# A graph layer's edge sum on one core: two quads of edges are summed behind all other late nodes instead of one, the lists are cleared in 4 transfers instead of 14

## The chip, the core and the metric

The kernel runs on one core of a Trainium2 chip. Five engines work side by side, each on its own queue in order: PE (matrix products), DVE (elementwise work and reductions), ACT (activation functions), POOL (here almost only gathers by index) and SP (here only issues transfers). PE writes to PSUM, of which the program keeps four banks in a list. The metric is the time of one execution in microseconds; lower is better.

## The reference

One layer of a message-passing network over 12,500 nodes with 128 features and 400,000 edges, sorted by destination, then a residual and a layer norm:

```python
rbf = exp(-(distances[:, None] - centers) ** 2 / (2.0 * width * width))
cut = 0.5 * (cos(pi * distances / CUTOFF) + 1.0) * (distances <= CUTOFF)
W = (silu(rbf @ fw1 + fb1) @ fw2 + fb2) * cut[:, None]
messages = (h[src] @ pw + pb) * W
agg = segment_sum(messages, dst, num_segments=num_atoms)
y = h + (silu(agg @ mw1 + mb1) @ mw2 + mb2)      # h is x
out = layernorm(x + y)                           # so layernorm(2 x + ...)
```

Edges whose length is over the cutoff add nothing, so the kernel first packs the others into lists.

## The kernel before

**Quads.** The packed edges are worked in 139 quads (`NL`) of 512 edges. Quad `q` goes through: four gathers of 128 rows each on POOL (`fetch`, L1074; in eight quads, `SINGLY`, one of the four is copied row by row by SP instead); a radial basis and a first product for two quads together (`basis`, `first`, `silu`, on ACT and PE); a second product into a PSUM bank (`second`, L1144 and L1147); DVE's product of that bank and the gathered rows (`message`, L1156 and L1158); a one-hot matrix of destinations (`place`, L1170); PE's product of both, which is the sum over edges (`sum_up`, L1190); and DVE's addition into the table `aggT` at a base that is read from a list (`add`, L1223). A quad of the first four lists has one window of sums, one of the later lists two, of 128 nodes at most.

**Nodes.** A group of up to four tiles of 128 nodes can be finished once all edges to it have been added: `node_first` (two products into a bank, L1233 and L1234, then silu on ACT, L1238), `node_second` (L344 and L347), `node_stats` on DVE (L1254, L1259), `deviations` (four small DVE instructions and a square root, L1266 to L1270), `scales` (L1277, L1278), `normalize` (L1289 on DVE or POOL, L1292 on ACT) and a store. A late node group is named by its first tile: 80 and 84 have four tiles, 88 two, 90 three, 93 two, 95 three (the last cut off at 84 nodes).

**The last quad.** The quads are not taken in the order of their lists. `quad_of` takes one quad out of the third list and puts it last: quad 138 of the order is number 26 of the lists (`LAST`). Its edges end in early nodes, and where the data allow it only in one tile of them, `END` (tile 3). So every node but those of `END` is complete before it, and after it only `END` has to be finished.

**Order.** The code is one long program, in which each engine executes its instructions as they were written. The main loop takes step `q` from 0 to 136: message, work on nodes (`nodes`), `second(q + 2)`, the sum, the bases, the one-hot of the next quad, the additions that `added` gives out, and `tail`. `tail` and `READY` say how many steps before the end each late group has its `node_first`. `last_step` writes out the two last quads by hand, the very last in four pieces of 128 edges, each multiplied and summed as its gather lands.

**Banks.** `bank()` takes the first bank of a list and `free.append` gives it back when the code that uses it has been written, not when it has run. Where three of the four banks are in use, the next user gets the bank that was just given back, and waits at run time for whatever still reads it.

```python
    def bank(own=None):
        while not free:
            go_on(next(c for c in held if c != own))
        return free.pop(0)
```

**Lists.** Before the packing scatters (L507) the lists in memory are cleared by SP (`clear_packed`, L229): 5 transfers, then 3, then 6.

Of the kernel before, what the change touches and what calls it, by code (L numbers as in the profile page):

```python
# [43 lines left out]
NL = 139  # L44
LAST = 26
AHEAD = 3
# [24 lines left out]
EARLY_US = 7  # L71
SINGLY = (22, 44, 62, 67, 86, 102, 118, 133)
A_ROW = .58
# [5 lines left out]
TAIL = {80: 4, 84: 4, 88: 2, 90: 3, 93: 2, 95: 3}  # L79
READY = {80: 9, 84: 6, 88: 5, 90: 4}  # L80
END = 3
# [5 lines left out]
def kernel(  # L87
# [60 lines left out]

    def load_x(t0, n=None):
        t = x4_sb[loaded[0] % X_BUFS]  # L150
        loaded[0] += 1
        node_dma(t0, t, x, False, n)
        x_sb[t0] = t
# [26 lines left out]
    def quad_of(q):  # L180

        return q if q < LAST or q >= NL else LAST if q == NL - 1 else q + 1

    def steps(k):

        return k if k <= LAST or k >= NL else k - 1

# [35 lines left out]
    def clear_packed(k, eng):  # L223
        a, b = CLEAR[k:k + 2]
        for i in range(LISTS if k == 0 else 3):
            v = packed[i, a:b].rearrange("(p w) -> p w", p=P)
            for w0 in range(0, (b - a) // P, 376):
                n = min(376, (b - a) // P - w0)
                eng.dma_start(v[:, w0:w0 + n], zero_i[:, :n])  # L229

# [593 lines left out]
    def unpack(c):  # L824
# [132 lines left out]
        if QB[c] <= LAST < QB[c + 1]:  # L957
            k = 2 * (LAST - QB[c])
            upto, that = (work.tile([64, 1], F32, name=n, bufs=1)[:np_] for n in ("upto", "that"))
            nc.vector.scalar_tensor_tensor(that, ident[:np_, k:k + 1], -1.0, ident[:np_, k + 1:k + 2],  # L960
                                           op0=OP.mult, op1=OP.subtract)
# [122 lines left out]
    def quads(o):  # L1084

        return [q for q in (2 * o, 2 * o + 1) if q < NL]

    def radial(o, lengths, eng=nc.sync):

        n = math.prod(lengths.shape) // QE  # L1090
        d = work.tile([P, QE], F32, name="d", bufs=3)
        v = lengths.rearrange("(o h) e -> o h e", o=1)
        eng.dma_start(d, v.to_broadcast([64, 2, QE]))
        d_of[o] = d, n

    next_o = [0]

    def radials(to):

        while next_o[0] < min(to, -(-NL // 2)):  # L1100
            o = next_o[0]
            if not all(chunk_of(q) in stored for q in quads(o)):
                break
            a, b = 2 * quad_of(quads(o)[0]), 2 * quad_of(quads(o)[-1]) + 2
            assert b - a == 2 * len(quads(o))
            radial(o, near_d[a:b].rearrange("(h t) e -> h (t e)", t=2))
            next_o[0] += 1
# [97 lines left out]

    def bases_of(q0, q1):

        _, v = nc.values_load_multi_w_load_instructions(
            base_i[0:1, 2 * quad_of(q0):2 * quad_of(q1 - 1) + 2], engines=[mybir.EngineType.DVE],
            min_val=0, max_val=N - min(wide(q) for q in range(q0, q1)),  # L1210
            skip_runtime_bounds_check_because="bases are destinations, and end in the table")
        for k in range(2 * (q1 - q0)):
            bases[q0 + k // 2, k % 2] = v[k]

    def added(q):

        return max((q - 2) // 2 * 2 if q < NL - 14 else q - 1 if q < NL - 4 else q, 0)

# [84 lines left out]
    def finish(every):  # L1303

        for t0 in every:
            load_x(t0)
# [5 lines left out]
            normalize(*ready.pop(0), on=range(QT))  # L1312

# [32 lines left out]
    def nodes(q):  # L1346
# [21 lines left out]
        if q == NL - 7:  # L1368
            st_of[3] = statistics()
            node_stats(80, st_of[3])  # L1370
        if q == NL - 4:
            node_stats(84, st_of[3][:, 4:])
        if q == NL - 3:
            node_stats(88, st_of[3][:, 8:])

    st_of, deep = {}, []

    def last_step(q, msg):

        assert not ready and not deep and not singles  # L1380
        bases_of(q, NL - 1)
# [6 lines left out]
        assert done_to(2 * q + 2) >= 95 * P  # L1388
        node_first(93)

# [5 lines left out]
        add(q)  # L1396
        node_first(95)
        last(1)
        normalize(*ready.pop(0))
        for n in (2, 3):  # L1400
            normalize(*ready.pop(0), on=range(n), v=nc.gpsimd)
        node_second(93)
        last(2)
        node_second(95)
        last(3)
        node_stats(93, st_of[1], lambda: add(NL - 1))
        node_first(END)
        node_stats(95, st_of[1][:, 2:])
        node_second(END)
        node_stats(END, st_of[1][:, 5:])  # L1410
        scales(*deviations([93, 95, END], st_of[1]))
        normalize(*ready.pop(0), on=(0, 1), v=nc.gpsimd)
        normalize(*ready.pop(0), on=(0, 1), eng=nc.scalar)
        normalize(*ready.pop(0), on=(0,))
        assert not ready

    def tail(q):

        for t0, k in READY.items():
            if q == NL - k:  # L1420
                assert done_to(2 * added(q + 1) + (2 if t0 > 88 else 0)) >= (t0 + TAIL[t0]) * P
                node_first(t0)
# [144 lines left out]
    for q in range(NL - 2):  # L1567
# [33 lines left out]
        if q == NL - 3:  # L1601
            st_of[1] = statistics()
            node_stats(90, st_of[3][:, 10:])
        if q == NL - 4:
            place(NL - 1)
            base_of(NL - 1)
            node_dma(END, end_sb, x, False)
            x_sb[END] = end_sb
        for k in now:
# [19 lines left out]
        elif counted and some is None and fetched[0] >= QT * NL:  # L1629
            some = nc.values_load(bad_i[0:1, 2:3], min_val=0, max_val=3 * E)  # L1630
    last_step(NL - 2, message(NL - 2))

    def more(q):

        fetch(-2, srci[:, 2 * q:2 * q + 2, :].rearrange("p r j -> p (r j)"))
        radial(-1, near_d[2 * q:2 * q + 2].rearrange("(o p) e -> o (p e)", o=1))
        basis(-1)
# [11 lines left out]
    def everything():  # L1649
        nc.vector.memset(aggT, 0.0)  # L1650
        def again(e0, seen):
# [20 lines left out]
            fetch(-2, idx)  # L1672
            radial(-1, edge_weight[ds(e0, QE)].rearrange("(o e) -> o e", o=1), nc.gpsimd)
            basis(-1)
# [64 lines left out]
```

## Time and profile before

| | us |
|---|---|
| three runs | 719.8, 721.39, 721.6 (median 721.39) |
| the profiled execution | 719.15 |
| its span, first to last instruction | 717.5 |
| busy in the span: PE, DVE, POOL, ACT | 590.3, 561.8, 536.4, 397.3 |

The profiled execution is 1.65 us longer than its span, and lies 2.24 us under the median of the runs. In the rows of the timeline the first number is the start in us from the span's start, the second the length; "x8" counts instructions merged into a row; a bracket gives the idle time ahead of it and what ended it.

### The profile page before, as it was taken

The page shows a single profiled execution, that of the slowest core. Times are in us where ns is not written, and L with a number is a line of the kernel's source. Part 1 is how long each engine was busy: PE and PEld are TensorE (multiplying, and loading weights), DVE is VectorE, ACT ScalarE, POOL GpSimd, SP SyncE. Part 2 cuts the span into 40 slices and gives each one's busy share as a digit, 9 for nine tenths or more (in the row PEclk, how much of TensorE's full clock was granted, in tenths as well). Part 3 has the DMA queues.
Part 4 walks back from the last instruction along what each step waited for, and adds up shares of the span by engine and source line. Part 5 has one row for each costly group of instructions (what it writes and reads, how often), then busy time and mean ns, then how long its engine had stood idle before and what let it go on. Part 6 is the DMA issues. An engine that isn't in the chain of part 4 may idle for free. (4 is left out here: it accounts for less than half of the span.)

```text
span 717.5 us, 13667 instructions
## 1 busy us (share of the span) xinstructions
PE 590.3 (82%) x3524; PEld 465.0 (65%) x3524; DVE 561.8 (78%) x1736; ACT 397.3 (55%) x564; POOL 536.4 (75%) x576
## 2 busy tenths in 40 slices
PE   6887877898889889888588896999987878878884
PEld 5775556776667667576466674787765655656663
DVE  8899799787988999899689895878655455565685
ACT  6557624563645566464348253858744833574474
POOL 7777777777777777777777777777777777777773
PEclk9999687997988999999979997999998999999998
DMA  8995442343334334343333343444433433244342
GB/s 263 348 324 174 149 128 75 87 137 100 98 86 121 97 95 108 97 128 83 94 106 113 98 119 103 137 127 135 136 97 99 148 92 114 84 141 134 96 130 91
DMA packets 53389, 91.35 MB, mean 127 GB/s; under 512 B 13856, under 2 KB 21120, under 8 KB 53306
## 3 DMA queue, kind: packets, MB, share of 16 engines
q1 hardware_dynamic: 34754, 53.20, 22.9%
q0 software_dynamic: 17840, 36.77, 19.8%
q8 instruction: 29, 0.48, 0.3%
q10 hardware_dynamic: 712, 0.46, 0.2%
q14 instruction: 54, 0.44, 0.2%
HBM read 74.59 MB, written 15.79 MB: 126 GB/s over the span
## 5 line engine op out<-in xcount | busy, mean ns | idle before, releaser
L1074 POOL DMA_INDIRECT quad<-proj,srci x421 | 400.6, 952 | 128.4 <-issue 97.6
L1147 PEld LDWEIGHTS bank<-fw_sb,s 128*128 128x128 f32 x1112 | 160.8, 208 | 66.5 <-issue 59.8
L1136 ACT ACTIVATE s<-ph 128x1024 f32<-128x1024 f32 x70 | 71.3, 1018 | 184.4 <-PE ph L1130 184.3
L1147 PE MATMUL bank<-fw_sb,s 128*128 128x128 f32 x1112 | 161.8, 293 | 0.0
L1130 PE MATMUL ph<-rbf,w_sb 102*128 102x512 f32 x278 | 147.1, 655 | 7.5 <-ACT rbf L1122 3.9
L1190 PEld LDWEIGHTS sums<-hot,msg 128*128 128x128 f32 x816 | 112.0, 204 | 54.9 <-issue 27.4
L1170 DVE TENSOR_SCALAR hot<-iota_n,dl,cut 128x80 f32<-128x80 f32 (+4 forms) x408 | 110.1, 344 | 23.6 <-PE sums L1190 21.7
L1190 PE MATMUL sums<-hot,msg 128*128 128x80 f32 (+4 forms) x816 | 113.7, 285 | 15.4 <-DVE msg L1156 7.7
L1144 PE MATMUL bank<-fb_b,ones_b 96*128 96x512 bf16 x139 | 56.1, 404 | 48.8 <-DVE msg L1158 29.8
L1074 POOL DMA_INDIRECT x<-proj,srci x79 | 75.0, 949 | 24.1 <-issue 19.8
L1158 DVE TENSOR_TENSOR msg<-bank,quad 128x512 f32<-128x512 f32 (+1 forms) x82 | 55.7, 679 | 39.4 <-DMA quad<-proj,srci 36.9
L1130 PEld LDWEIGHTS ph<-rbf,w_sb 102*128 102x128 f32 x278 | 52.8, 211 | 48.1 <-issue 38.8
L1223 DVE TENSOR_TENSOR aggT<-aggT,sums 128x80 f32 (+4 forms) x209 | 54.0, 258 | 32.5 <-PE bank L1234 11.7
L1121 ACT ACTIVATE rbf<-d,rbf_bias,rbf_scale 102x512 f32<-102x512 f32 x70 | 56.2, 803 | 14.8 <-DMA d<-near_d 14.7
L1074 POOL DMA_INDIRECT quad<-in_x_dram,srci x48 | 47.6, 992 | 14.8 <-issue 11.9
L347 PEld LDWEIGHTS bank<-pw_sb,xT 128*128 128x128 f32 (+1 forms) x292 | 42.0, 207 | 8.0 <-issue 4.0
L1122 ACT ACT_TABLE_LOAD x35 | 44.9, 1283 | 0.6
L1136 ACT ACT_TABLE_LOAD x35 | 44.9, 1283 | 0.6
L1122 ACT ACTIVATE rbf<-rbf 102x512 f32<-102x512 f32 x70 | 44.1, 630 | 1.5
L1190 PE MATMUL sums<-quad,quad 128*128 128x104 f32 (+3 forms) x296 | 40.9, 281 | 3.9 <-DVE quad L1158 3.9
L1170 DVE TENSOR_SCALAR quad<-iota_n,dl,cut 128x104 f32<-128x104 f32 (+3 forms) x148 | 40.5, 348 | 3.9 <-issue 2.8
L1158 DVE TENSOR_TENSOR quad<-bank,quad 128x512 f32<-128x512 f32 (+2 forms) x40 | 25.2, 632 | 23.4 <-DMA quad<-proj,srci 16.1
(282 smaller groups left out, 803.0 us busy)
## 6 DMA issues: line engine op xcount, KB each, us to landing
d<-near_d SPq DMA_DIRECT2D x70, 256.0 KB
dl<-proj SPq DMA_DIRECT2D x1024, 0.5 KB
x<-in_x_dram SPq DMA_DIRECT2D x45, 256.0 KB
quad<-proj,srci POOLq DMA_INDIRECT x421
proj<-hp SPq DMA_DIRECT2D x24, 256.0 KB
out_dram<-x SPq DMA_DIRECT2D x21, 256.0 KB
r_d<-in_edge_weight_dram SPq DMA_DIRECT2D x5, 256.0 KB
r_dst<-in_dst_dram SPq DMA_DIRECT2D x5, 256.0 KB
```

The lines of the kernel that those rows point to most:

```text
L347: nc.tensor.matmul(to[:m, k, :], lT[:, k * P:k * P + m], w, start=False, stop=(k == a + c - 1))
L1074: ins = nc.gpsimd.indirect_dma_start(out=got[:, j, :], out_offset=None, in_=proj if table is None else table, in_offset=bass.IndirectOffse ...
L1121: nc.scalar.activation(rbf[:u], d[:u], AF.Square, bias=rbf_bias[:u], scale=rbf_scale[:u])
L1122: nc.scalar.activation(rbf[:u], rbf[:u], AF.Exp, scale=-1.0 / (2.0 * width * width))
L1130: nc.tensor.matmul(ph[:, h, :], w1_sb[:2 * KR, h, :], rbf[:2 * KR], start=True, stop=True)
L1136: nc.scalar.activation(s[:, :n], ph[:, :n], AF.Silu)
L1144: nc.tensor.matmul(pu, ones_b[:, :P], bias_b["fb2"].rearrange("k j f -> k (j f)"), start=True, stop=False)
L1147: nc.tensor.matmul(pu[:, j * H:(j + 1) * H], s[:, j * P:(j + 1) * P], fw2_sb, start=False, stop=(j == QT - 1))
L1158: nc.vector.tensor_mul(msg[:, a:b, :], pu_of[q].rearrange("p (j f) -> p j f", j=QT)[:, a:b, :], got_of[q][:, a:b, :])
L1170: nc.vector.tensor_scalar(hot[:, j, :wide(q)], iota_n[:, :wide(q)], dl[:, at[0], at[1]], cut[:, at[0], at[1]], op0=OP.is_equal, op1=OP.mult)
L1190: ins = nc.tensor.matmul(pa[:, k * W:k * W + wide(q)], msg[:, j, :], hot[:, j, :wide(q)], start=(j % n == 0), stop=(j % n == n - 1))
L1223: nc.vector.tensor_add(to, to, pa[:, k * W:k * W + wide(q)])
```

## The change

- Two quads, numbers 25 and 26 of the lists, now come last (`N_LAST = 2`, as quads 137 and 138); every other quad from 25 on moves up by one place. Both have one window of 80 nodes. Their edges that go beyond `END` would be counted as misses, as before for one.
- So all late nodes are complete after quad 136. `READY` starts group 84 one step earlier, 88 and 90 too, and 93 and 95, which were in `last_step`, in the main loop. Statistics and second products move with them.
- `last_step` has one set of `deviations` over the 14 tiles of 84, 88, 90, 93 and 95, ahead of quad 137's sum. After the last quad only `END` is left: its double input is added by PE into the bank, the statistics are taken from the bank, and a `bn_aggr` replaces the four small instructions.
- `END`'s input is loaded one step earlier, and doubled by ACT in place.
- The lists are cleared by one transfer for all lists together: 1, then 1, then 2.
- Three numbers in `SINGLY` follow the shifted order. In code that runs only when edges were missed, transfers move from SP's queue to POOL's.

```diff
-LAST = 26
+LAST = 25
+N_LAST = 2
-READY = {80: 9, 84: 6, 88: 5, 90: 4}
+READY = {80: 9, 84: 7, 88: 6, 90: 5, 93: 4, 95: 3}
...
-        return q if q < LAST or q >= NL else LAST if q == NL - 1 else q + 1
+        late = q - (NL - N_LAST)
+        return q if q < LAST or q >= NL else LAST + late if late >= 0 else q + N_LAST
...
-        for i in range(LISTS if k == 0 else 3):
-            v = packed[i, a:b].rearrange("(p w) -> p w", p=P)
-            for w0 in range(0, (b - a) // P, 376):
-                n = min(376, (b - a) // P - w0)
-                eng.dma_start(v[:, w0:w0 + n], zero_i[:, :n])
+        m = LISTS if k == 0 else 3
+        v = packed[:m, a:b].rearrange("s (p w) -> p s w", p=P)
+        for w0 in range(0, (b - a) // P, 376):
+            n = min(376, (b - a) // P - w0)
+            eng.dma_start(v[:, :, w0:w0 + n], zero_i[:, None, :n].to_broadcast([P, m, n]))
...
-        return max((q - 2) // 2 * 2 if q < NL - 14 else q - 1 if q < NL - 4 else q, 0)
+        return max((q - 2) // 2 * 2 if q < NL - 14 else q - 1 if q < NL - 5 else q, 0)
...
-    def last_step(q, msg):
+    def last_step(q):
...
-        roots = deviations([84, 88, 90], st_of[3][:, 4:])
+        node_second(95)
+        node_stats(95, st_of[1][:, 11:])
+        msg = message(q)
+        nc.scalar.activation(warm, half_pi, AF.Sqrt)
+        roots = deviations([84, 88, 90, 93, 95], st_of[1])
         nc.scalar.activation(warm, half_pi, AF.Silu)
...
-        keep_busy(5)
+        keep_busy(3)
         sum_up(q, msg)
...
         scales(*roots)
         add(q)
-        node_first(95)
+        keep_busy(2)
         last(1)
...
+        normalize(*of[95], on=range(3))
+        normalize(*of[88])
+        normalize(*of[90])
+        keep_busy(2)
         last(2)
+        normalize(*of[93], on=range(2))
+        normalize(*of[84], on=range(4), v=nc.gpsimd)
+        keep_busy(1)
+        pz, py = bank(), bank()
...
+        nc.tensor.matmul(py[:, :H], ident, end_sb[:, 0, :], start=False, stop=False)
         last(3)
+        add(NL - 1)
+        nc.tensor.matmul(pz[:, :P], mw1_sb, aggT[:, END * P:(END + 1) * P], start=False, stop=True)
...
+        nc.scalar.activation(zs, pz[:, :P], AF.Silu)
+        nc.tensor.matmul(py[:, :H], zs, mw2_sb, start=False, stop=True)
...
+        nc.vector.bn_stats(st, py[:, :H])
+        nc.vector.bn_aggr(mv, st)
...
+        nc.scalar.activation(dev[:, 0:1], mv[:, 1:2], AF.Sqrt, bias=eps)
+        nc.vector.reciprocal(dev[:, 1:2], dev[:, 0:1])
+        nc.vector.tensor_scalar(end_sb[:, 0, :], py[:, :H], mv[:, 0:1], dev[:, 1:2],
+                                op0=OP.subtract, op1=OP.mult)
...
+        node_dma(END, end_sb, out, True)
...
         if q == NL - 4:
             keep_busy(2)
+            node_second(90)
         if q == NL - 3:
-            node_second(90)
+            node_second(93)
...
+        if q == NL - 5:
             node_dma(END, end_sb, x, False)
-            x_sb[END] = end_sb
+            nc.scalar.activation(end_sb, end_sb, AF.Copy, scale=2.0)
```

What this moves on the engines is seen in three places.

On PE, around the sums of quads 132 and 133 (the two rows `sums<-hot`), before: `fb_b` and `fw_sb` mark the second product of a quad, `aggT,mw_sb` the first product of a node group, here of group 84.

```order
L1190 MATMUL sums<-hot_1071,msg_1076 128x128 x4
L1144 LDWEIGHTS ones_b
L1144 MATMUL bank_169<-fb_b,ones_b 128x512
L1147 MATMUL bank_169<-fw_sb,s 128x128 x4
L1130 MATMUL ph<-rbf,w_sb 128x512
L1190 MATMUL sums<-hot_1190,msg_1218 128x128 x4
L1233 LDWEIGHTS mb_b
L1233 MATMUL bank_170<-ones_b,mb_b 128x512
L1234 MATMUL bank_170<-aggT,mw_sb 128x512
```

The same place now:

```order
L1197 MATMUL sums<-hot_1065,msg_1070 128x128 x4
L1231 LDWEIGHTS mb_b
L1231 MATMUL bank_169<-ones_b,mb_b 128x512
L1232 MATMUL bank_169<-aggT,mw_sb 128x512
L1151 LDWEIGHTS ones_b
L1151 MATMUL bank_169<-fb_b,ones_b 128x512
L1154 MATMUL bank_169<-fw_sb,s 128x128 x4
L1137 MATMUL ph<-rbf,w_sb 128x512
L1197 MATMUL sums<-hot_1184,msg_1208 128x128 x4
```

Group 84's first product has moved from behind quad 133's sum to ahead of quad 135's second product, which uses the same bank (`bank_169`) right after it.

On ACT, from the square roots ahead of the last groups on, now (`zs` are the silus of groups 88 and 90, `x` the tiles that are normalized, `end` the tile of `END`):

```order
L1631 ACT_TABLE_LOAD
L1631 ACTIVATE warm<-half_pi 128x1
L1236 ACTIVATE zs<-bank_167 128x256
L1290 ACTIVATE x_89<-x_89,by,rs 128x128 x4
L1290 ACTIVATE x_90<-x_90,by,rs 128x128 x4
L1625 ACTIVATE end<-end 128x128
L1236 ACTIVATE zs<-bank_170 128x384
L1290 ACTIVATE x_91<-x_91,by,rs 128x128 x4
```

Before, the first silu here was group 84's, group 88's stood in the place of the `end` row, and group 90's behind eight more normalized tiles.

On SP, the transfers of that time, now:

```order
L179 DMA out_dram<-x_89 128x512
L179 DMA out_dram<-x_90 128x512
L179 DMA x_89<-in_x_dram 128x256
L179 DMA end<-in_x_dram 128x128
L179 DMA out_dram<-x_91 128x512
L179 DMA out_dram<-x_92 128x512
```

`END`'s load has moved from behind all loads of the late groups to behind the load into `x_89`, which waits until that tile's store, two rows above, has landed.

More of the change, by code (lines that the diff above doesn't have):

```diff
@@ L71 @@
 EARLY_US = 7
-SINGLY = (22, 44, 62, 67, 86, 102, 118, 133)
+SINGLY = (22, 43, 62, 66, 86, 102, 118, 133)
 A_ROW = .58
@@ L1088, in radial @@
     def radial(o, lengths, eng=nc.sync):
-        n = math.prod(lengths.shape) // QE
         d = work.tile([P, QE], F32, name="d", bufs=3)
-        v = lengths.rearrange("(o h) e -> o h e", o=1)
-        eng.dma_start(d, v.to_broadcast([64, 2, QE]))
-        d_of[o] = d, n
+        for h, v in enumerate(lengths):
+            v = v.rearrange("(o h) e -> o h e", o=1)
+            if len(lengths) == 1:
+                eng.dma_start(d, v.to_broadcast([64, 2, QE]))
+            else:
+                eng.dma_start(d[h::2], v[:, 0, :].to_broadcast([64, QE]))
+        d_of[o] = d, sum(math.prod(v.shape) for v in lengths) // QE
     next_o = [0]
@@ L1204, in base_of @@
             bases[q, k] = v[0]
[L1206 to L1213, printed above, removed]
     def added(q):
-        return max((q - 2) // 2 * 2 if q < NL - 14 else q - 1 if q < NL - 4 else q, 0)
+        return max((q - 2) // 2 * 2 if q < NL - 14 else q - 1 if q < NL - 5 else q, 0)
     def add(q, ks=(0, 1)):
@@ L1305, in finish @@
         for t0 in every:
[L1306 removed]
+            load_x(t0, eng=nc.gpsimd)
             st = statistics()
@@ L1311, in finish @@
             scales(*deviations([t0], st))
-            normalize(*ready.pop(0), on=range(QT))
+            normalize(*ready.pop(0), on=range(QT), eng=nc.gpsimd)
     def finish_four(e):
@@ L1420, in tail @@
             if q == NL - k:
-                assert done_to(2 * added(q + 1) + (2 if t0 > 88 else 0)) >= (t0 + TAIL[t0]) * P
+                a = added(q + 1)
+                assert a == NL - N_LAST or done_to(2 * quad_of(a)) >= (t0 + TAIL[t0]) * P
                 node_first(t0)
```

62 lines of the change are left out of this document (28 added, 34 removed).

## The prediction

> **What bounds the kernel now.** I read the groups of POOL's instructions first, since the page shows POOL busy in equal tenths from the first slice to the last but one:
>
> ```profile
> L1074 POOL DMA_INDIRECT quad<-proj,srci x421 | 400.6, 952 | 128.4 <-issue 97.6 <-DMA quad<-proj,srci 9.4 <-DVE aggT L1223 4.0
> ...
> L507 POOL DMA_INDIRECT packed<-line,at_i x7 | 7.0, 994 | 2.7 <-issue 1.2 <-DVE base_i L653 0.9 <-DVE bank L528 0.3
> ```
>
> 421 of the gathers keep POOL for 529 us (400.6 + 128.4), 0.95 each and 0.30 between, and the gap is the same whatever released it. So POOL never waits long for anybody; its stream sets when the last quad's rows arrive. The change leaves the number of gathers alone, so what it can move is the end. The chain of waits begins there, with the last gather of quad 137:
>
> ```profile
> 698.62 2.93 DMA quad<-proj,srci
> ```
>
> That one lands at 701.55, and DVE's timeline has that quad's message at 701.67, in step with it:
>
> ```profile
> 699.59 0.55 DVE L1254 SCALAR_TENSOR_TENSOR x<-x,bank 128x384 f32<-128x384 f32 x1
> 700.17 0.68 DVE L1259 BATCH_NORM_STATS2 st<-x 128x6 f32<-128x128 f32 x3
> ...
> 701.67 0.69 DVE L1158 TENSOR_TENSOR msg<-bank,quad 128x512 f32<-128x512 f32 x1
> ...
> 705.60 0.77 DVE L1158 TENSOR_TENSOR quad<-bank,quad 128x128 f32<-128x128 f32 x3
> ...
> 712.84 0.34 DVE L1289 TENSOR_SCALAR end<-end,rs,by 128x128 f32<-128x128 f32 x1
> ```
>
> Quad 138's last piece is multiplied by 706.38 (705.60 + 0.77), and END's tile is normalized from 712.84. On SP's timeline its store is the last issue, at 713.96, 3.54 before the span ends at 717.5:
>
> ```profile
> 690.72 1.88 SPq L178 DMA_DIRECT2D out_dram<-x  x2
> 693.13 0.34 SPq L178 DMA_DIRECT2D x<-in_x_dram  x1
> ...
> 713.96 0.40 SPq L178 DMA_DIRECT2D out_dram<-end  x1
> ```
>
> So the end is 706.38 for the last piece, and 7.58 from there to that store. I cost the change in these two parts. Two more views carry it, ACT's timeline and PE's:
>
> ```profile
> 684.75 0.60 ACT L1136 ACTIVATE s<-ph 128x512 f32<-128x512 f32 x1 [1.84 <-PE ph L1130]
> 685.36 1.28 ACT L1270 ACT_TABLE_LOAD   x1
> 686.66 0.50 ACT L1270 ACTIVATE dev<-v,eps 128x16 f32<-128x16 f32 x2
> 687.17 1.28 ACT L1614 ACT_TABLE_LOAD   x1
> 688.47 0.20 ACT L1614 ACTIVATE warm<-half_pi 128x1 f32<-128x1 f32 x1
> 688.58 0.58 ACT L1238 ACTIVATE zs<-bank 128x512 f32<-128x512 f32 x1
> 689.05 3.17 ACT L1292 ACTIVATE x<-x,by,rs 128x128 f32<-128x128 f32 x8
> 692.13 0.36 ACT L1238 ACTIVATE zs<-bank 128x256 f32<-128x256 f32 x1
> ...
> 709.45 0.28 ACT L1238 ACTIVATE zs<-bank 128x128 f32<-128x128 f32 x1 [0.74 <-PE bank L344]
> 709.75 1.28 ACT L1270 ACT_TABLE_LOAD   x1
> ```
>
> ```profile
> 682.58 0.38 PE L1144 MATMUL bank<-fb_b,ones_b 96*128 96x512 bf16 x1
> 682.80 1.05 PE L1147 MATMUL bank<-fw_sb,s 128*128 128x128 f32 x8
> 683.69 1.02 PE L1130 MATMUL ph<-rbf,w_sb 102*128 102x512 f32 x2
> 684.55 1.05 PE L1190 MATMUL sums<-hot,msg 128*128 128x128 f32 x8
> 685.44 0.38 PE L1233 MATMUL bank<-ones_b,mb_b 96*128 96x512 bf16 x1
> 686.89 1.12 PE L1234 MATMUL bank<-aggT,mw_sb 128*128 128x512 f32 x2 [1.07 <-DVE aggT L1223]
> 687.86 0.38 PE L1144 MATMUL bank<-fb_b,ones_b 96*128 96x512 bf16 x1
> ...
> 692.54 0.38 PE L1144 MATMUL bank<-fb_b,ones_b 96*128 96x512 bf16 x1 [0.53 <-ACT zs L1238]
> ...
> 694.09 1.05 PE L1190 MATMUL sums<-quad,quad 128*128 128x128 f32 x8
> ```
>
> Two things are to be seen. At 692.54 PE waits 0.53 us for a silu: quad 137's second product was given the bank that the silu of group 88 (692.13 to 692.49) was still reading. And ACT needs 3.83 us from quad 138's silu (684.75) to the next one (688.58), because two table loads and two square roots lie between.
>
> **Part one: when the last piece is multiplied.** All times are on the profiled execution's clock.
>
> *To second(136), +3.4.* Group 84's first product now stands ahead of second(135), at 682.58, and both use one bank. It takes 0.38 and 1.12 with a small gap, to 684.2; its silu 0.58, to 684.85; only then second(135) runs (1.11, from 682.58 to 683.69 in the rows) and quad 138's first product (1.02), to 687.0. ACT's silu for quad 138 starts at 687.0 instead of 684.75, 2.25 late, and the same 3.83 puts the next silu, now group 88's, at 690.8. It ends at 691.2, and second(136), in that bank too, starts there: before, at 687.86.
>
> *To the sum of quad 135, +7.4.* ACT then normalizes eight tiles as before (3.17), to 694.35, and reaches the doubling of END, whose load must have landed. SP issues that load behind a load into a tile whose store must land first. The store needs four of the eight tiles, at 692.85. Before, the store went out at 690.72 and the load behind it at 693.13, 2.41 later; so that load goes out at 695.25, and END's 0.45 after it, at 695.7. How long it takes to land no row shows: the store's 2.41 and the gather's 2.93 are the nearest, I take 2.6. So 698.3, the doubling 0.28 (as the silu of such a tile), and group 90's silu 698.6 to 699.1. Its input is there by 695.1: second(136) ends at 692.4, quad 134's sum at 693.5 (1.05), the two additions at 694.1, the product at 695.1. The doubling thus holds ACT for 3.5 us, and PE with it, since second(137) gets group 90's bank. On SP two stores and a load are queued behind END's load; nobody needs them before group 95's statistics. Then second(137) 1.11, two dummy products 0.5, group 90's second product 0.83 (three quarters of 1.11): quad 135's sum starts at 701.5, before at 694.09.
>
> *To the message of quad 137, +10.6.* From here each quad's sum stands behind the next late group. DVE takes group 90's statistics, 0.55 and 0.68, a one-hot of about 1.0, and adds quad 135 in 0.6: 704.55. PE: group 93's first product 0.5, second(138) 1.11, its second product 0.55, quad 136's sum to 707.85, added by 708.5. Group 95: product 0.9, silu 0.55, second product and its end 1.1, to 711.0; statistics as for group 90, 1.23, to 712.25. Only then quad 137's message, before at 701.67 on landing.
>
> *To the last piece, +10.7.* Message 0.62, deviations 0.7, square root 0.35, scales 0.42, one addition 0.3, then pieces of 0.25 with five normalized tiles of 0.32 between: the last is multiplied at 717.05. Before it was at 706.38.
>
> **Part two: from there to the store, -3.9.** Sum 0.4, addition 0.3, product 0.55, silu 0.33, product 0.55: 719.2. Statistics 0.3, then `bn_aggr`, which no row shows; DVE's small instructions run from 0.17 (`by`, `dif`) to 0.3, I take 0.25: 719.7. Beside it the table load starts when the silu ends, at 718.6, and is done at 719.9, so the missing dummy costs 0.2. Square root 0.25, reciprocal 0.2, the normalized tile 0.35: the store at 720.75. That is 3.7 where 7.58 stood, since PE's second products, four small DVE instructions and POOL's tiles no longer lie in it.
>
> In the row at 685.36 the square root follows 0.02 after the load has ended. [...]
>
> **Edits with nothing to give.** The clears leave SP 10 issues:
>
> ```profile
> L229 SPq DMA_DIRECT2D packed<-zero_i x14: 356/438/481, 14.6 to 84.5; - x14
> ```
>
> 10 at 0.44 are 4.4 us, on a queue that POOL does not wait for: the scatters' idle time is 2.7 over seven, 2.1 of it the usual gap, and the longest of it ended by DVE. Zero, at most 0.6 gained. The moved singles keep their count; zero, within 0.3 either way.
>
> **Sum.** +10.7 - 3.9 = +6.8 us. The profiled execution would take 719.15 + 6.8 = 726.0; it lies 2.24 under the median, and on the median of 721.39 the forecast is 728.2. Its own range, with the load's landing, the small instructions, the sequencers' register loads and the runs' spread: 726.5 to 730.2.
>
> **Rivals.** A measurement of this kernel tells about 0.3% (2.2 us) from no change.
>
> - *The late groups fit into PE's and ACT's gaps (faster).* PE is busy for 590.3 of 717.5 us, so the late groups might cost nothing. Then the last piece stays at 706.38 and only part two counts: 717.5. It decides while the last piece is less than 1.7 us late (3.9 less the 2.2); from 6.1 late on the change is slower. Against it: the bank wait at 692.54 shows that silus do hold PE, and one group now comes per step. 0.05.
> - *The doubling does not hold ACT* (END's load lands before 695.1, so SP would not have waited for the store): 3.45 less, 724.8. Against it, the row at 693.13. 0.11.
> - *Neither the doubling nor the banks hold, only the chain of late groups:* the same working with those waits left out has quad 135's sum at 695.9, quad 137's message at 706.6 and the store at 715.1, +1.1, 722.5. 0.05.
> - *The clears' issue time reaches the end:* 4.4 less than the forecast, 723.8. 0.03. [...]
>
> **How the numbers follow.** The forecast keeps 0.76. Faster 0.05 is the first rival, the same 0.05 the third, slower 0.90 the rest. The range takes in the second and fourth rivals and the forecast's own: 723.8 to 730.2.
>
> **What would show it.** In the profile after: POOL's last gather still near 703.6; ACT idle for 3 to 4 us ahead of the doubling, ended by END's load; PE idle for silus ahead of second(135), (136) and (137); quad 137's message near 712 with its rows long landed; the store under 4 us behind the last piece. I am wrong if that message starts less than 6 us after its landing, or if POOL's stream ends elsewhere.

## The result, and the profile after

| | before | after |
|---|---|---|
| median of seven runs, us | 720.87 (719.8 to 723.48) | 727.15 (725.71 to 731.18) |
| ratio of the runs | | 1.0086, 95% interval 1.0061 to 1.011 |
| span of the profiled execution | 717.5 | 725.5 |
| POOL's last gather starts | 703.62 | 704.08 |
| last piece of quad 138 multiplied (done) | 706.37 | 717.91 |
| `END`'s store issued | 713.96 | 721.90 |

The changed kernel is slower, by 6.2 us by the ratio and by 8.0 between the two profiled spans (that of before lies 1.7 under its median). POOL's gathers first. Their group and the last of them in the timeline:

```profile
L1077 POOL DMA_INDIRECT quad<-proj,srci x421 | 401.1, 953 | 128.3 <-issue 98.7 <-DMA quad<-proj,srci 9.1 <-DVE aggT L1221 4.9
704.08 0.94 POOL L1077 DMA_INDIRECT quad<-proj,srci  x1 [0.30 <-issue]
```

401.1 + 128.3 is 529.4, as before; only 0.46 of the 8.0 has come up before the end. The clears, as SP's issues:

```profile
L231 SPq DMA_DIRECT2D packed<-zero_i x4: 385/410/475, 14.4 to 85.1; - x4
L509 POOL DMA_INDIRECT packed<-line,at_i x7 | 7.0, 995 | 2.7 <-issue 0.9 <-DVE base_i L655 0.9 <-DVE aggT L1221 0.6
```

SP has 4 issues of 0.41 for 14 of 0.44, some 4.5 us less, and the scatters behind them have not moved: the idle time of the seven is 2.7, as before. The loss lies in the end. ACT's timeline:

```profile
697.76 0.31 ACT L1625 ACTIVATE end<-end 128x128 f32<-128x128 f32 x1 [3.85 <-DMA end<-in_x_dram]
697.98 0.47 ACT L1236 ACTIVATE zs<-bank 128x384 f32<-128x384 f32 x1
```

For 3.85 us ACT does nothing but wait for `END`'s load, ahead of the doubling; group 90's silu (697.98) stands behind it. SP's queue tells why the load is so late:

```profile
692.39 1.88 SPq L179 DMA_DIRECT2D out_dram<-x  x2
694.85 0.34 SPq L179 DMA_DIRECT2D x<-in_x_dram  x1
695.25 0.42 SPq L179 DMA_DIRECT2D end<-in_x_dram  x1
...
721.90 0.33 SPq L179 DMA_DIRECT2D out_dram<-end  x1
```

The load in front of it (694.85) goes out 2.46 behind the store at 692.39, whose tile it overwrites. That row holds two stores: SP issues the second only when ACT has normalized its tiles (the eight end at 693.91), and is done with it at 694.27 (692.39 + 1.88); only the remaining 0.58 is for the landing of the first. On PE the wait shows once more, and something behind it:

```profile
690.88 0.38 PE L1151 MATMUL bank<-fb_b,ones_b 96*128 96x512 bf16 x1 [1.15 <-ACT zs L1236]
691.09 1.05 PE L1154 MATMUL bank<-fw_sb,s 128*128 128x128 f32 x8
...
698.50 0.59 PE L1151 MATMUL bank<-fb_b,ones_b 96*128 96x512 bf16 x1 [3.84 <-ACT zs L1236]
698.88 1.91 PE L1154 MATMUL bank<-fw_sb,s 128*128 128x128 f32 x8
...
703.04 1.44 PE L1197 MATMUL sums<-quad,quad 128*128 128x128 f32 x8
```

second(136) and second(137) both wait for silus. But the eight products of second(137) take 1.91, those of second(136) 1.05, with the same shapes. The table of stretches shows the granted clock; its record changes at 697.01 and at 703.84, and each stretch is 3.41 long (columns: from, to and length; busy time, with instructions in brackets, of PE, its weight loads, DVE, ACT and POOL; clock; DMA share and GB/s):

```profile
693.60:697.01 3.41, 1.06 (x3) 0.40 (x3) 2.62 (x9) 0.30 (x1) 2.50 (x4) 1.00 0.72 237
697.01:700.42 3.41, 1.92 (x9) 1.83 (x9) 0.00 (x0) 2.66 (x8) 2.50 (x4) 0.50 0.28 70
700.42:703.84 3.42, 3.42 (x15) 2.79 (x15) 0.55 (x1) 1.10 (x3) 2.74 (x3) 0.50 0.72 222
703.84:707.25 3.41, 1.96 (x13) 1.28 (x12) 2.95 (x12) 0.38 (x1) 0.94 (x1) 1.00 0.27 78
```

Behind PE's idle time of 3.84 its clock is at 0.50 for 6.83 us (697.01 to 703.84), just where the chain needs it. DVE's timeline carries the rest of the chain to the end:

```profile
705.39 0.59 DVE L1221 TENSOR_TENSOR aggT<-aggT,sums 128x128 f32 x2
...
713.77 0.67 DVE L1165 TENSOR_TENSOR msg<-bank,quad 128x512 f32<-128x512 f32 x1
...
717.63 0.28 DVE L1165 TENSOR_TENSOR quad<-bank,quad 128x128 f32<-128x128 f32 x1
...
720.20 0.30 DVE L1420 BATCH_NORM_STATS2 st_end<-bank 128x6 f32<-128x128 f32 x1 [1.44 <-PE bank L1418]
720.53 0.18 DVE L1421 BATCH_NORM_AGGREGATE mv_end<-st_end 128x2 f32<-128x6 f32 x1
...
721.46 0.41 DVE L1425 TENSOR_SCALAR end<-bank,mv_end,dev_end 128x128 f32<-128x128 f32 x1
```

Quad 137's message stands at 713.77. The last of its gathers was issued four before the last one, near 699.1, so with the 2.93 of the row shown of before it landed near 702.0, an estimate; the message is some 11.8 late. Last piece to store takes 3.99 where 7.58 stood. So 11.5 lost on the way to the last piece, 3.6 won behind it.

### The profile page after: what moved, and what is told of

It reads as the page before. It is cut to its first block, busy times and chain, and to the rows that moved or that the text cites. A ratio compares the mean times of both kernels' runs of the same rounds, so it can differ in the third digit from the quotient of the medians.

```text
span 725.5 us, 13638 instructions
## 1 busy us (share of the span) xinstructions
PE 592.6 (82%) x3529; PEld 465.7 (64%) x3529; DVE 561.6 (77%) x1735; ACT 397.9 (55%) x566; POOL 535.6 (74%) x573
## 5 line engine op out<-in xcount | busy, mean ns | idle before, releaser
L1077 POOL DMA_INDIRECT quad<-proj,srci x421 | 401.1, 953 | 128.3 <-issue 98.7
L349 PE MATMUL bank<-pw_sb,xT 128*128 128x128 f32 (+1 forms) x292 | 43.7, 298 | 0.3 <-ACT xT L1013 0.3
L1197 PE MATMUL sums<-quad,quad 128*128 128x80 f32 (+3 forms) x296 | 40.2, 278 | 4.3 <-DVE quad L1165 4.1
```

Source lines behind the costliest of these rows:

```text
L349: nc.tensor.matmul(to[:m, k, :], lT[:, k * P:k * P + m], w, start=False, stop=(k == a + c - 1))
L1077: ins = nc.gpsimd.indirect_dma_start(out=got[:, j, :], out_offset=None, in_=proj if table is None else table, in_offset=bass.IndirectOffse ...
L1197: ins = nc.tensor.matmul(pa[:, k * W:k * W + wide(q)], msg[:, j, :], hot[:, j, :wide(q)], start=(j % n == 0), stop=(j % n == n - 1))
```

## The experiments

POOL's last gather lies between 702.97 and 705.93 in these profiled runs. So beside each ratio stands the time from its start to the issue of `END`'s store, read in each kernel's timelines of POOL and SP.

| kernel | ratio to the kernel before (95%) | last gather to store, us |
|---|---|---|
| before | 1 | 10.34 |
| after | 1.0086 (1.0061 to 1.011) | 17.82 |
| `END`'s load early | 1.0040 (1.0025 to 1.0054) | 13.79 |
| message's bank first | 1.0080 (1.0064 to 1.0095) | 16.54 |
| both | 1.0026 (1.0010 to 1.0041) | 12.69 |
| dummy products on PE | 1.0051 (1.0036 to 1.0066) | 15.65 |
| `END` finished the old way | 1.0091 (1.0076 to 1.0105) | 18.50 |
| clears alone, in the kernel before | 1.0003 (0.9988 to 1.0018) | |
| both, and sums first on PE | 1.0047 (1.0029 to 1.0064) | 13.82 |
| the same, pieces first | 1.0016 (1.0001 to 1.0032) | 13.99 |

**`END`'s load early.**

```diff
+        if q == NL - 9:
+            node_dma(END, end_sb, x, False)
         for k, t0 in enumerate(TAIL):
...
         if q == NL - 5:
-            node_dma(END, end_sb, x, False)
             nc.scalar.activation(end_sb, end_sb, AF.Copy, scale=2.0)
```

> The changed kernel (median 727.15, store at 721.90 in its profile), with END's input loaded four steps earlier, ahead of group 80's load; the doubling on ACT stays where it is. Theory (the doubling holds ACT and then PE): ACT no longer waits 3.85 us ahead of the doubling, group 90's silu starts near 694.7 instead of 697.98, second(137) near 695.3 instead of 698.50, and since PE is then idle under 1 us there, its clock stays at 1.00 instead of 0.50, which gives another 1.5. The store comes at 717.3, 4.6 earlier: 722.5. Rival (only the chain of late groups holds, the doubling's wait lies beside it): within 0.5 of the changed kernel, 727. Rival (the wait moves on to the banks): 1 to 2 earlier, 725.5.

Measured: 4.0 less from the last gather to the store, and 3.3 us (0.0046 of 720) by the ratios, whose intervals lie apart. ACT, then PE, then the stretches of PE's clock:

```profile
693.16 0.29 ACT L1626 ACTIVATE end<-end 128x128 f32<-128x128 f32 x1
694.05 0.49 ACT L1236 ACTIVATE zs<-bank 128x384 f32<-128x384 f32 x1 [0.60 <-PE bank L1232]
```

```profile
699.97 0.70 PE L1232 MATMUL bank<-aggT,mw_sb 128*128 128x256 f32 x2 [1.83 <-DVE aggT L1221]
...
700.87 1.51 PE L1154 MATMUL bank<-fw_sb,s 128*128 128x128 f32 x8
```

```profile
697.91:701.32 3.41, 1.57 (x10) 0.95 (x8) 2.97 (x12) 0.38 (x1) 2.50 (x4) 1.00 0.65 186
701.32:704.73 3.41, 3.41 (x18) 3.35 (x17) 1.60 (x6) 1.65 (x4) 2.54 (x3) 0.50 0.37 105
```

The doubling no longer waits and the silu follows its own input: the doubling's wait, with the slow stretch that stood behind it, is shown to be the largest single part of the loss. The clock was expected to stay whole. It did not: PE now waits 1.83 ahead of group 93's first product, for quad 135's addition, and falls to 0.50 one stretch later. Measured from POOL's last gather, quad 135's sum starts 5.5 earlier than in the changed kernel and the last piece is done 4.0 earlier; the 1.5 between the two were lost from quad 136's message to its addition, where the new slow stretch lies. That the store still came where it was expected (717.32 for 717.3) is in part luck, since that gather started 0.55 earlier in this run.

**The message's bank first.**

```diff
-            free.append(pu_of.pop(q))
+            free.insert(0 if q >= NL - 8 else len(free), pu_of.pop(q))
```

> The changed kernel, but in the last eight steps the bank that a message gives back goes to the front of the list, so that second takes it and not the bank that a late group's silu still reads. Theory (banks hold PE): second(136) no longer waits for group 84's silu, nor second(137) for group 90's behind the doubling; second(137) runs near 694.5 instead of 698.50. ACT still waits for END's load, so group 90's second product and what follows it stay near 698.4. The store comes 3 to 4 earlier: 723.5. Rival (the doubling alone holds and the banks cost nothing): under 1 earlier, 726.5.

Measured: 1.3 less in the profile, where 3 to 4 were expected, and 0.0006 between ratios whose intervals overlap. ACT, then PE, then DVE's last piece, then four stretches of PE's clock:

```profile
695.96 0.31 ACT L1625 ACTIVATE end<-end 128x128 f32<-128x128 f32 x1 [3.71 <-DMA end<-in_x_dram]
```

```profile
692.48 0.38 PE L1151 MATMUL bank<-fb_b,ones_b 96*128 96x512 bf16 x1
...
696.70 0.32 PE L346 MATMUL bank<-mb_b,ones_b 96*128 96x384 bf16 x1 [2.51 <-ACT zs L1236]
...
697.52 1.06 PE L1197 MATMUL sums<-quad,quad 128*128 128x128 f32 x8
```

```profile
714.10 0.27 DVE L1165 TENSOR_TENSOR quad<-bank,quad 128x128 f32<-128x128 f32 x1
```

```profile
692.25:695.66 3.41, 1.94 (x13) 1.27 (x12) 1.88 (x8) 0.00 (x0) 2.71 (x3) 1.00 0.67 196
695.66:699.08 3.42, 2.00 (x16) 1.71 (x15) 1.26 (x5) 3.12 (x9) 2.60 (x3) 1.00 0.22 59
...
709.32:712.73 3.41, 2.17 (x15) 1.32 (x13) 3.17 (x16) 1.59 (x4) 0.29 (x1) 1.00 0.03 7
712.73:716.14 3.41, 3.40 (x14) 2.49 (x13) 1.64 (x7) 2.46 (x7) 1.60 (x4) 0.50 0.31 100
```

second(137) does run early, at 692.48. Group 90's own second product (696.70) still stands ahead of quad 135's sum in PE's queue and waits for the same silu, but for 2.51 instead of 3.84, and second(137) no longer lies behind that wait. Up to the last piece the gain is 2.9 (done at 714.37, 10.95 behind POOL's last gather, for 13.83 in the changed kernel). From there to the store it takes 5.59, for 3.99 in the changed kernel: PE's clock is at 0.50 from 712.73 on, where the last sums and `END`'s products are. So the bank is worth more than the 1.15 ahead of second(136), and 1.6 of the 2.9 went again at a slow clock that the expectation did not have.

**Both.** The two edits above together.

> Both edits, END's input loaded earlier and the message's bank taken first. Theory (these two waits are nearly the whole loss of part one): the store at 715.1, 6.8 earlier than in the changed kernel: 720.4, level with the kernel before. Rival (one wait behind the other, taking away both gives no more than the larger): 722.5. Rival (the late chain gives way to arrival): the last piece is multiplied about 3 us behind the last gather as in the kernel before, store at 711.2, 716.5.

Measured: 5.1 less in the profile and 4.3 us by the ratios, between the theory and the first rival. Up to the last piece the two edits gain 4.0 and 2.9 alone, and 5.1 together (done at 712.55, 8.70 behind the last gather): the waits overlap. That 5.1 is also near the 4.0 and 1.3 of the whole profiles is chance, as the 1.3 has the slow end of that run in it. The kernel stays 0.26% above the kernel before. What quad 135's addition, and PE behind it, still wait for is seen on DVE and PE:

```profile
695.70 0.55 DVE L1252 SCALAR_TENSOR_TENSOR x<-x,bank 128x384 f32<-128x384 f32 x1 [0.85 <-ACT x L1290]
696.28 0.68 DVE L1257 BATCH_NORM_STATS2 st<-x 128x6 f32<-128x128 f32 x3
696.88 1.00 DVE L1177 TENSOR_SCALAR quad<-iota_n,dl,cut 128x80 f32<-128x80 f32 x4
697.83 0.61 DVE L1221 TENSOR_TENSOR aggT<-aggT,sums 128x128 f32 x2
```

```profile
695.44 1.06 PE L1197 MATMUL sums<-quad,quad 128*128 128x128 f32 x8
...
698.49 0.70 PE L1232 MATMUL bank<-aggT,mw_sb 128*128 128x256 f32 x2 [1.89 <-DVE aggT L1221]
```

Quad 135's sum is there by 696.5, but DVE first finishes group 90's statistics and writes the one-hots of quad 138; it adds at 697.83, and PE idles 1.89 for that.

**Dummy products on PE**, in the changed kernel, 14 into the 3.84 us and 6 ahead of group 93's first product.

```diff
+        if q == NL - 4:
+            keep_busy(14)
         if q + 2 < NL:
             second(q + 2)
...
+                if t0 == 93:
+                    keep_busy(6)
                 node_first(t0)
```

> The changed kernel with dummy products added on PE where it idles: 14 ahead of second(137), into the 3.84 us, and 6 ahead of group 93's first product. Theory (PE runs at half its clock after that idle time, 0.50 from 697.0 to 703.8, and this is late work on the chain): second(137) still starts at 698.5, but its eight products take 1.05 instead of 1.91 and quad 135's sum starts at 701.2 instead of 703.04; the store comes 1.5 to 2.1 earlier: 725.3. Rival (DVE's statistics and one-hots hold quad 135's addition anyway): under 0.5, 727. Rival (the dummies stand in the way of the products behind them): slower by 0.5 to 1.

Measured: 2.2 less in the profile and 2.5 us by the ratios (the intervals just overlap). ACT, PE and the stretches:

```profile
696.63 0.31 ACT L1629 ACTIVATE end<-end 128x128 f32<-128x128 f32 x1 [3.96 <-DMA end<-in_x_dram]
696.85 0.47 ACT L1236 ACTIVATE zs<-bank 128x384 f32<-128x384 f32 x1
```

```profile
693.26 3.19 PE L1446 MATMUL ph<-mb_b,ones_b 96*128 96x512 bf16 x14
697.37 0.38 PE L1151 MATMUL bank<-fb_b,ones_b 96*128 96x512 bf16 x1 [0.92 <-ACT zs L1236]
697.58 1.05 PE L1154 MATMUL bank<-fw_sb,s 128*128 128x128 f32 x8
...
699.74 1.06 PE L1197 MATMUL sums<-quad,quad 128*128 128x128 f32 x8
```

```profile
693.57:696.98 3.41, 2.88 (x14) 1.19 (x13) 1.47 (x6) 0.35 (x2) 2.50 (x4) 1.00 0.62 180
696.98:700.39 3.41, 3.02 (x24) 2.74 (x24) 0.45 (x1) 3.41 (x9) 2.58 (x3) 1.00 0.36 105
```

Nothing but useless work was added, ACT waits for `END` as long as ever, and the kernel is faster. From group 90's silu to the start of quad 135's sum, ahead of which only the 14 stand, it is 2.89 (696.85 to 699.74) against 5.06 (697.98 to 703.04). So the slow clock was worth 2.2 us of the loss.

**`END` finished the old way**, in the changed kernel. The copy by ACT (times 1) keeps the wait for the load.

```diff
-            nc.scalar.activation(end_sb, end_sb, AF.Copy, scale=2.0)
+            nc.scalar.activation(end_sb, end_sb, AF.Copy, scale=1.0)
...
         last(3)
         add(NL - 1)
-        nc.vector.bn_stats(st, py[:, :H])
-        nc.vector.bn_aggr(mv, st)
...
+        x_sb[END] = end_sb
+        node_first(END)
+        node_second(END)
+        node_stats(END, st)
+        nc.scalar.activation(warm, half_pi, AF.Sqrt)
+        scales(*deviations([END], st))
+        normalize(*ready.pop(0), on=(0,))
```

> The changed kernel with END finished in the old way: second product into a bank of its own after the silu, doubling and addition by DVE, statistics from SBUF, four small DVE instructions, a dummy square root ahead of the last one, scales. END's input is still touched by ACT at the same place (multiplied by 1), so that the wait there stays. Theory (most of part two came from groups 93 and 95 leaving the end, the short END path is the smaller share): an addition of 0.3, four small instructions of 0.15 in place of an aggregation of 0.18, a further small one, less 0.2 of the table load that is hidden again: 1.0 later than the changed kernel, 728.1. Rival (the whole 3.6 lies in END's own path): 730.7. Rival (no difference, the table load's exposed part weighs as much as what is saved): 727.2.

Measured: from the last piece (done at 717.13) to the store (721.68) 4.55, against 3.99; the ratios, 1.0091 and 1.0086, do not tell them apart. DVE's timeline:

```profile
719.35 0.29 DVE L1252 SCALAR_TENSOR_TENSOR end<-end,bank 128x128 f32<-128x128 f32 x1 [1.44 <-PE bank L349]
...
720.00 0.16 DVE L1264 TENSOR_TENSOR dif<-st 128x1 f32<-128x1 f32 x1
...
720.38 0.16 DVE L1267 TENSOR_TENSOR v<-both_m,dif 128x1 f32<-128x1 f32 x1
```

So the folding and the aggregation are worth 0.56 of the 3.6 of part two, where 1.0 was expected. The other 3.0, by subtraction, came from groups 93 and 95 leaving the end.

**The clears alone**, in the kernel before.

```diff
-        for i in range(LISTS if k == 0 else 3):
...
-                eng.dma_start(v[:, w0:w0 + n], zero_i[:, :n])
+            eng.dma_start(v[:, :, w0:w0 + n], zero_i[:, None, :n].to_broadcast([P, m, n]))
```

> The kernel before with nothing changed but the clears, 4 transfers instead of 14. Theory (nothing waits for SP's issue time there): within 0.6 of the kernel before, 720.9. Rival (the issue time reaches the end): 4.4 faster, 716.5. Rival (each transfer of all lists lands later than the first of five did, and the first scatter waits for it): slower by 0.5 to 2.

Measured: 719.73 against 719.8. Nothing waits for them.

**Sums first on PE.** Both edits; quads 135's and 136's sums ahead of the second products of groups 90 and 93; 4 dummy products ahead of the first products of 93 and 95.

```diff
-            node_second(90)
-        if q == NL - 3:
-            node_second(93)
         sum_up(q, msg)
+        if q == NL - 4:
+            node_second(90)
+        if q == NL - 3:
+            node_second(93)
```

> END's input early and the message's bank first, as in the run with both (721.53, store at 716.54), and further: the sums of quads 135 and 136 stand ahead of the second products of groups 90 and 93 on PE instead of behind them, and 4 dummy products ahead of the first products of groups 93 and 95 hold PE's clock. Theory (a chain of sum, addition, first product for each of the last late groups sets the end, and everything put into it counts): 0.9 for each of the two second products and 1.0 of the slow clock less, together 2.5, store near 714.0, 719.0. Rival (DVE's statistics of group 90 and the one-hots hold the additions, so PE's order is worth nothing): 721.

Measured: a miss. It gains nothing on both edits alone: 1.0047 against 1.0026, with intervals that overlap, and 1.1 longer in the profile. DVE's timeline:

```profile
698.53 0.55 DVE L1252 SCALAR_TENSOR_TENSOR x<-x,bank 128x384 f32<-128x384 f32 x1 [1.82 <-issue]
...
700.70 0.61 DVE L1221 TENSOR_TENSOR aggT<-aggT,sums 128x128 f32 x2
```

The statistics of group 90 read the second product that now comes later (done at 698.44; the bracket names no releaser), and in DVE's queue they still stand ahead of quad 135's addition. From that quad's message to its addition done it is 7.2 us (694.11 to 701.31), with both edits 6.3 (692.17 to 698.44). The rival named in the expectation was right in its reason: reordering one queue alone moved the wait into the other. The four dummy products did not help either: PE still waited 1.96 ahead of group 93's first product, and behind that wait the eight products of second(138) took 1.91 (from 702.80), where those of second(137) had taken 1.05 (from 695.22).

**Pieces first.** As that run, and quad 137's message, its sum and one piece ahead of group 95's statistics.

```diff
-        node_second(95)
-        node_stats(95, st_of[1][:, 11:])
         msg = message(q)
+        sum_up(q, msg)
+        node_second(95)
...
+        last(0)
+        node_stats(95, st_of[1][:, 11:])
+        add(q)
```

> As the run before, and in the last step quad 137's message, its sum and the first piece of quad 138 stand ahead of group 95's statistics. Theory (the late chain no longer stands before the two last quads, they wait only for their gathers): the last piece is multiplied near 709 and the store comes near 712.8, 717.8, some 2 under the kernel before (719.8 on this chip). Rival (the fourteen tiles that are then normalized last set the end by their own stores): no gain over the run before, 719.

Measured: 1.0016, the nearest to the kernel before of all orders of the changed kernel that were timed well, and not under it. Against both edits alone the intervals overlap. The theory failed: in the profile, an execution 1.9 above the median of its runs, the last piece is done at 713.28 where 709 was expected, and the store comes no sooner behind the last gather than in the run before. The late chain now stands between the first piece and the second, which is multiplied at 710.57, behind group 95's statistics and the deviations.

**Three more orders, and all together.** In these last two series of runs all kernels, the one before with them, took 1,012 to 1,021 us: POOL's gathers stood still at times, 2.78 ahead of the one at 974.52 and 4.91 ahead of the one at 982.87 in the profile of the last of these runs, where most have 0.30 (their gaps sum to 293.4 in the row below, of the third of these runs, for 128.3 above), so that ratios are known to half a per cent at best. That is too wide to settle any of the expectations below.

```profile
L1077 POOL DMA_INDIRECT quad<-proj,srci x421 | 400.9, 952 | 293.4 <-issue 149.5
```

*Adds first*: DVE adds quads 135 and 136 before it takes the statistics of groups 90 and 93.

```diff
-        if q == NL - 4:
-            node_stats(90, st_of[1][:, 6:])
...
         for k in now:
...
             add(k)
+        if q == NL - 4:
+            node_stats(90, st_of[1][:, 6:])
```

> As the run with the pieces first (quads' sums ahead of the second products), and now DVE too adds quads 135 and 136 before it takes the statistics of groups 90 and 93 and writes the one-hots of quad 138; no dummy products ahead of group 93, 2 ahead of group 95. Theory (in the two runs before, DVE's queue held the additions: its statistics of group 90 waited 1.8 for the second product that had been moved behind the sum): quad 135's addition is done 2.5 to 3 earlier, measured from POOL's last gather, PE no longer idles 2 ahead of group 93 and keeps its clock; store near 714.5 for a last gather at 704.1, some 2 under the kernel before. Rival (something else holds the additions): level with the run before, 0.2% over the kernel before.

Measured: 0.9986 (0.9933 to 1.0039).

*End first*: the last two pieces ahead of most normalized tiles.

```diff
         scales(*roots)
+        last(2)
         normalize(*of[95], on=range(3))
...
-        last(2)
...
         last(3)
+        normalize(*of[93], on=range(2))
```

> As the run before, and quad 138's last two pieces stand ahead of most of the fourteen normalized tiles on DVE, POOL's four tiles first. Theory (with the additions early, the last pieces wait for nothing but their gathers and what stands before them on DVE): last piece near 5 behind POOL's last gather, store 1 earlier than in the run before, some 2.5 to 3 under the kernel before. Rival (the fourteen tiles' stores then end last): the same as the run before.

Measured: 1.0016 (0.9974 to 1.0059).

*Both, with dummies*:

```diff
+                if t0 == 93:
+                    keep_busy(8)
                 node_first(t0)
```

> The run with both edits (END's input early, the message's bank first), and 8 dummy products on PE ahead of group 93's first product, where it idled 1.9 before its clock fell to 0.50. Theory (the slow clock is the third part of the loss beside the doubling and the banks): the clock stays at 1.00 to the end, second(138) takes 1.05 and not 1.83, the store comes 1.3 earlier than with both edits, level with the kernel before within 0.2%. Rival (the slow stretch lies beside DVE's work): no difference from the run with both edits, 0.26% over the kernel before.

Measured: 0.9997 (0.9948 to 1.0046).

*All together*, with the orders on PE and DVE, the two edits and the dummy products, and besides:

```diff
-            free.insert(0 if q >= NL - 8 else len(free), pu_of.pop(q))
+            free.insert(0 if NL - 8 <= q < NL - 3 else len(free), pu_of.pop(q))
...
+        if q == NL - 3:
+            keep_busy(3)
...
-        if q == NL - 4:
+        if q == NL - 3:
             place(NL - 1)
```

> The changed kernel with what the runs point to put together: END's input early; the message's bank first in the steps before the last two; the sums of quads 135 and 136 ahead of the second products on PE; the additions of 135 and 136 ahead of statistics and one-hots on DVE; group 95's statistics and the deviations of the fourteen tiles as in the changed kernel, ahead of the last pieces, of which the last now stands ahead of two normalized tiles; dummy products where PE would idle. Theory (END's wait, the banks, the order in front of the additions and the slow clock are the loss, and with them away the end waits for the last gather again): quad 136's message near its landing, the last piece about 4 behind POOL's last gather (13.8 in the changed kernel, 2.75 in the kernel before), the store 4 behind that, the span 2 under the kernel before's, ratio 0.997. Rival (fourteen tiles and their stores, all behind the last statistics, set the end): level with the kernel before, ratio 1.000 to 1.002. Rival (the chain of late groups is as long with any order): as with both edits, 1.0026.

Measured: median 1011.74 (992.45 to 1020.51) against 1013.83 (1003.63 to 1023.47) for the kernel before; no verdict follows. Whether this order beats the kernel before is open.

## Why the prediction was right

It said slower by 6.8, 728.2; the measured 727.15 and the 6.2 of the ratio lie inside its range. By its own steps (us of the profiled execution; the last column is measured less predicted):

| step | predicted | measured | |
|---|---|---|---|
| second(136) starts | 691.2 | 690.88 | -0.3 |
| doubling of `END` starts | 698.3 | 697.76 | -0.5 |
| second(137) starts | 699.1 | 698.50 | -0.6 |
| quad 135's sum starts | 701.5 | 703.04 | +1.5 |
| quad 135 added | 704.55 | 705.98 | +1.4 |
| quad 137's message | 712.25 | 713.77 | +1.5 |
| last piece multiplied | 717.05 | 717.91 | +0.9 |
| last piece to store | 3.7 | 3.99 | +0.3 |
| store | 720.75 | 721.90 | +1.2 |

- *To second(136)*: right, and for the named cause, the bank (1.15 ahead of it).
- *To the sum of quad 135*: the wait for `END`'s load is as foreseen, 3.85 for 3.5, and it is the largest part: taking it away gives 3.3 to 4.0. Two things in this step failed. The first is a size: from second(137)'s start to the sum the prediction counted 2.4, at the durations of the kernel before (1.05 for eight products), and it took 4.5, with PE's clock at 0.50 behind its idle time (1.91 for eight products). The prediction saw that PE would be held for 3.5 us and did not ask what that does to its clock; the dummy products show the price, 2.2, which the 3.3 to 4.0 above overlap: both runs take away the same slow stretch. The 3.84 here stands ahead of a stretch at 0.50, and so does the 1.83 with `END`'s load early. The second is a reason: PE was said to be held because second(137) gets group 90's bank. With the bank free PE still waited for the same silu, 2.51 for 3.84, ahead of group 90's second product; the bank lengthens the wait but is not its cause.
- *To the message of quad 137* and *to the last piece*: the delay was carried on as said, group by group; the late start of 1.5 shrank to 0.9, because the deviations, scales and pieces took 4.14 from the message to the last piece done where 4.8 were counted.
- *Part two*: -3.6 for -3.9. The aggregation takes 0.18 for 0.25; the last normalized tile 0.41 for 0.35. The table load ends at 720.92 (719.64 + 1.28) and the square root starts at 720.93, 0.01 behind it and 0.22 behind the aggregation: the exposed part was sized right. The experiment adds which edit it was: the short path of `END` gives 0.56, the rest is that two groups have left the end.
- *Clears*: zero, shown. (Of the numbers in `SINGLY` two have moved, 44 to 43 and 67 to 66, not three.)
- *Rivals*: that the late groups fit the gaps is refuted by the spans. That the doubling does not hold ACT is refuted by the run with the early load. Banks and doubling do not tell the whole: without both, 1.9 us stay by the ratio, where the third rival's working left 1.1 to the chain of late groups. That this chain, with DVE's order and the slow clock in it, holds these is read from one profile; how much each of the two has of it is open, since the run for it (both, with dummies) knows its ratio to half a per cent only.

Between the profile's +8.0 and the ratio's +6.2 lies the profiled execution of before, 1.7 under its median; the prediction took a difference of profiles onto a median. On the profiles its 6.8 is 1.2 too little, on the timed runs 0.6 too much; that it came this close to the timed runs is in part luck.

## What to carry to other kernels

When an instruction on a strict queue is made to wait for a load, follow that load through its own queue to what it stands behind, here two stores that wait for normalized tiles and a load that waits for one of them to land; issuing it four steps earlier cost nothing and gave back half of the loss. Work that is moved earlier is not free because its engine has gaps: ask which waits it puts into each queue in front of the one chain that sets the end. Reordering one queue alone only moved the wait here; whether reordering every queue that chain crosses pays was not shown. And when a change will leave PE idle, price a slow stretch behind it too: here 6.83 us at 0.50 stood behind a wait of 3.84. With 14 dummy products in that wait the clock was at 1.00 and 2.2 us came back; behind 4 ahead of a wait of 1.96, eight products still took 1.91.

## What had not been expected of the hardware

In the stretches printed above, 3.41 us each, PE's granted clock was 1.00 or 0.50. It was at 0.50 in the stretch behind one in which PE was busy for 1.06 (the changed kernel, from 693.60), behind one with 1.57 whose longest wait was 1.83 (`END`'s load early, from 697.91), and behind one with 2.17 whose longest wait was 1.24 (the message's bank first, from 709.32). It was at 1.00 behind 2.88 and 3.02 (the dummy products, from 693.57 and 696.98), but also behind 1.94 and 2.00 (the message's bank first, from 692.25 and 695.66), the two stretches into which one wait of 2.51 fell in parts. Two stretches at 0.50 that were filled to the end had 1.00 behind them (3.42 in the changed kernel, 3.41 with `END`'s load early), and one had 0.50 (3.40, the last row with the message's bank first). So neither the busy time of a stretch nor the longest wait puts these cases in order: 2.17 and a wait of 1.24 stand ahead of 0.50, 1.94 and a wait of 2.51 ahead of 1.00. What sets the clock was not shown.
